# A gated attention and expert block: another order for the work of batch 0

## The chip, the core and the metric

The kernel runs on one core of a Trainium2 chip. The core has a matrix engine (TensorE, PE in the tables; its weight loads are listed apart as PEld), three engines for elementwise work (VectorE or DVE, ScalarE or ACT, GpSimd or POOL), and SyncE (SP), which here only issues transfers. Each engine carries out its own instructions in the order in which the program emits them; semaphores make one wait for another. Transfers are issued by SP, ACT or POOL and carried out by 16 DMA engines. The metric is the device time of one execution in microseconds; lower is better.

## The reference

Eight batches of 256 tokens of width 512, all in fp32. Each batch goes through an attention block and an expert block, both gated:

```python
x = x + jnp.tanh(g_xattn[0]) * _L0_xattn_ref(_layernorm(x, axis=-1), ctx_2048, ...)
x = x + jnp.tanh(g_ffn[0]) * _L0_ffn_ref(_layernorm(x, axis=-1), ...)

# attention: 32 query heads, 8 key heads of width 16, two sources of keys
q = _heads(jnp.concatenate([ssm_states, hidden_states], axis=-1) @ Wq, H)
k, v = _heads(hidden_states @ Wk, HK), _heads(hidden_states @ Wv, HK)
ssm_k, ssm_v = _heads(ssm_states @ Wsk, HK), _heads(ssm_states @ Wsv, HK)
...
scores = jnp.einsum('bhqd,bhkd->bhqk', q, k) / np.sqrt(D) + bias[None]   # ALiBi
scores = jnp.where(mask[None, None], scores, -jnp.inf)                  # 64 keys back, both sources
o = jnp.einsum('bhqk,bhkd->bhqd', jax.nn.softmax(scores, axis=-1), v)   # then @ Wo

# experts: 128 of them, each a mix of 8 basis products; top 4 a token
basis = jax.nn.silu((xt @ w_gate).reshape(T, K, I)) * (xt @ w_up).reshape(T, K, I)
mixed = jnp.einsum('tek,tki->tei', mix[topk_idx], basis)
out = jnp.einsum('teh,te->th', jnp.einsum('tei,ih->teh', mixed, w_down), topk_w * expert_scale[topk_idx])
out = out + jax.nn.silu(xt @ shared_w_gate) * (xt @ shared_w_up) @ shared_w_down
```

## The kernel before

**Stages of a batch.** `project(b)` makes keys, queries and values (PE, evicted by ACT). `attention(b)` does the softmax and the product with the values. `tail(b, t)`, for each half t of 128 tokens, multiplies by wo, adds the residual, normalises, transposes into hT and computes the router's choice. `feed_forward(b)` does the eight basis products and the shared expert. Stages of neighbouring batches run beside each other.

**The order** of all instructions is written by a planner in Python that stands at the end of the function (`start`, `run`). Every stage is a generator; it yields costs, and `start(gen, length, at, total)` places it on an axis where one batch is 1.0: a yield of cost c moves the stage on by c x length / total. `run` resumes whichever stage is due first, and what that stage then emits goes next into the engines' queues. Nothing is reordered afterwards, so a due time alone decides what stands behind what on each engine. Before the planner begins, loads, constants and the norm of batch 0 are emitted outside of this manual order.

**The softmax** of a batch has 8 groups of two query blocks, 16 units u in all (u = 2i + j). `score(i)` computes a group's scores for four pairs of key heads into four PSUM banks. A unit then takes `soften` for each pair (DVE: adds nbias, row extreme, L589), the exponential (ACT, L603), `divide` one unit later (DVE reciprocal, L612, then POOL, L615), `turn` two units later (DVE transpose, L623). After four units `values` (PE, L645) multiplies by vbd, and `take` (ACT, L662) evicts. `values` writes a spare part of the banks of a group's scores. A unit is emitted in four parts, with a yield of 1.0 behind each: the start, and steps 0, 1 and 2. The buffers `pr` that hold a unit's weights are three.

**vbd** holds the values on diagonals. `put_values` (ACT, L455) writes vpad, and `diagonals(qd, eng)` copies it by four transfers of 128 KB for each of four qd (L449), issued by `eng`.

**The feed-forward** multiplies two-by-two blocks with seven products instead of eight, which needs four sums of weight blocks for each k. For batch 0 they are formed once, stored to DRAM by `keep` (L848) and loaded from there by later batches. `first_sums(k)` forms the four sums of one k on POOL (`sub`, L844) while batch 0's attention runs: for k = 2, 3, 0, 1. Those of k = 4 to 7 are formed inside batch 0's feed-forward, two on DVE and two on POOL (`late`, `more`, L969). `load_gu` (L332) loads the weights, from SP.

**Banks.** Scores use a pool of four banks; batch 0's later groups also take two of the three feed-forward banks (`gu0` to `gu2`). One more bank (`one`) goes from user to user by `hold` and `give`.

## Time and profile before

| | us |
|---|---|
| median of three runs | 1043.92 (1040.56 to 1044.18) |
| profiled execution, its time | 1039.71 |
| profiled execution, its span | 1037.9 |
| PE busy in the span | 999.2 (96%) |
| DVE, ACT, POOL busy | 582.1, 420.5, 439.7 |
| first feed-forward matmul | 102.85 |

The span counts from the first to the last recorded instruction. The page gives each engine's busy time, then the chain of work that ended last, followed back from the end, then groups of instructions by source line. A row of a timeline has the start, the time from the first to the last of its instructions, engine, line, operation, output and inputs, and in brackets the idle time before it and what ended that. PE's ends are modelled, so neighbouring PE rows may overlap a little. In a group of PE matmuls the count is twice that of the source: each fp32 product is issued as two.

### The profile page before, as it was taken

What the parts mean: (1) busy time and instruction counts of PE and PEld (TensorE: products, weight loads), DVE (VectorE), ACT (ScalarE), POOL (GpSimd) and SP (SyncE); (2) the same over time, 40 slices, a digit from 0 to 9 for tenths busy, and PEclk for the clock granted to TensorE, in tenths of its full rate; (3) what the DMA queues carried; (4) which work ended last, traced back from release to release, by engine and by line L of the source; (5) the groups of instructions that cost most, each with busy time, mean ns of one, the idle gap of its engine ahead of it and who ended that gap; (6) DMA issues with size and microseconds to landing.
All of it is one profiled execution on the core that took longest, in us unless ns stands there. A gap on an engine that the chain in (4) does not pass through costs nothing.

```text
span 1037.9 us, 26745 instructions
## 1 busy us (share of the span) xinstructions
PE 999.2 (96%) x10072; PEld 793.6 (76%) x10072; DVE 582.1 (56%) x2185; ACT 420.5 (41%) x1608; POOL 439.7 (42%) x860
## 2 busy tenths in 40 slices
PE   6789989999999999999999999999999999999998
PEld 5657877867788688886878868787788868777885
DVE  1565666747554575536755467544756457754452
ACT  3452554426441464315543256423554136431220
POOL 3666456605542265413644136521454216540340
PEclk9889999999999999999999999999999999999999
DMA  8833964549543693527745386444954368553880
GB/s 254 217 109 115 234 186 150 174 129 283 163 137 111 169 300 123 159 98 191 263 138 157 107 235 217 144 136 125 278 163 144 112 166 258 167 174 120 263 277 20
DMA packets 111104, 180.80 MB, mean 174 GB/s; under 512 B 12160, under 2 KB 34176, under 8 KB 110976
## 3 DMA queue, kind: packets, MB, share of 16 engines
q1 hardware_dynamic: 108480, 176.22, 55.7%
q10 hardware_dynamic: 2112, 1.84, 0.5%
q8 instruction: 79, 1.29, 0.5%
q0 software_dynamic: 384, 1.05, 0.5%
q14 instruction: 49, 0.40, 0.1%
HBM read 149.69 MB, written 12.58 MB: 156 GB/s over the span
## 4 chain that ended last, share of the span: by engine, by line
PE 83%; DVE 8%; ACT 2%; DMA 2%; issue 2%; POOL 1%; SPq 1%; ACTq 0%; POOLq 0%; DVEq 0%
PE m L891 32%; PE ps L1025 10%; PE pq L512 8%; PE sc L645 5%; PE pd L1088 5%; PE po L758 5%; PE sc L576 5%; PE pd L1071 3%; PE pv L532 2%; PE pk L493 2%; DVE pr L589 2%; PE pl L789 1%; DVE pt L623 1%; ACT pr L603 1%; DMA w<-in_L_ffn_w_up 1%
## 5 line engine op out<-in xcount | busy, mean ns | idle before, releaser
L615 POOL TENSOR_SCALAR pr<-pr,rd 128x192 f32<-128x192 f32 (+2 forms) x512 | 206.5, 422 | 271.1 <-DVE rd L612 257.9
L603 ACT ACTIVATE pr<-pr,nm 128x192 f32<-128x192 f32 (+2 forms) x512 | 218.6, 430 | 109.8 <-DVE nm L589 73.8
L891 PE MATMUL m<-w,sT 128*128 128x256 f32 x1024 | 252.7, 381 | 0.1
L589 DVE CUSTOM_DVE_ANT_1 pr<-sc,nbias 128x192 f32<-128x192 f32 (+2 forms) x512 | 153.5, 322 | 122.9 <-PE sc L576 108.7
L891 PEld LDWEIGHTS m<-w,sT 128*128 128x128 f32 x1024 | 194.3, 191 | 27.7 <-issue 1.0
L891 PE MATMUL m<-w,hT 128*128 128x256 f32 x768 | 204.1, 388 | 0.0
L891 PEld LDWEIGHTS m<-w,hT 128*128 128x128 f32 x768 | 139.8, 191 | 24.2 <-issue 5.4
L964 POOL TENSOR_TENSOR mixed<-mixed,th 128x256 f32<-128x256 f32 x112 | 82.0, 732 | 177.3 <-DVE th L959 175.7
L1025 PE MATMUL ps<-hT,w 128*128 128x256 f32 x512 | 117.6, 381 | 0.0
L623 DVE STREAM_TRANSPOSE pt<-pr 128x768 f32<-128x768 f32 (+2 forms) x128 | 111.4, 871 | 3.3 <-POOL prob L798 1.9
L1025 PEld LDWEIGHTS ps<-hT,w 128*128 128x128 f32 x512 | 95.2, 190 | 14.7 <-issue 2.9
L603 ACT ACTIVATION_READ_ACCUMULATOR pr<-pr,nm 128x1 f32 x512 | 97.8, 191 | 0.0
L645 PEld LDWEIGHTS sc<-pt,vbd 64*32 64x32 f32 x5120 | 61.8, 106 | 27.5 <-issue 12.2
L645 PE MATMUL sc<-pt,vbd 64*32 64x96 f32 (+2 forms) x5120 | 70.9, 229 | 7.1 <-DMA vbd<-vpad 3.5
L576 PE MATMUL sc<-kT,qT 32*128 32x192 f32 (+2 forms) x1024 | 67.8, 343 | 6.3 <-DVE nm L589 6.0
L927 POOL TENSOR_TENSOR m<-m,u 128x256 f32<-128x256 f32 x64 | 47.7, 745 | 55.9 <-DVE u L926 47.0
L576 PEld LDWEIGHTS sc<-kT,qT 32*128 32x128 f32 x1024 | 48.2, 188 | 27.6 <-DVE nm L589 9.2
L949 DVE TENSOR_TENSOR gate<-u,m 128x256 f32<-128x256 f32 x64 | 26.4, 413 | 67.5 <-PE m L891 67.5
L854 ACT ACTIVATE th<-m 128x256 f32<-128x256 f32 x64 | 24.7, 386 | 96.6 <-DVE up L937 94.5
L854 ACT ACTIVATE th<-gate 128x256 f32<-128x256 f32 x64 | 26.5, 415 | 87.4 <-DVE gate L949 87.4
L758 PE MATMUL po<-wo,oT 128*128 128x512 f32 x128 | 57.7, 594 | 0.3 <-DVE cf L832 0.3
L512 PE MATMUL pq<-ctT,wq 128*128 128x256 f32 x224 | 54.2, 385 | 2.8 <-ACT kT L500 2.8
(129 smaller groups left out, 1212.8 us busy)
## 6 DMA issues: line engine op xcount, KB each, us to landing
w<-s SPq DMA_DIRECT2D x232, 256.0 KB, 3.3
w<-in_L_ffn_w_gate SPq DMA_DIRECT2D x132, 256.0 KB, 3.1
w<-in_L_ffn_w_up SPq DMA_DIRECT2D x74, 256.0 KB, 4.0
vbd<-vpad SPq DMA_DIRECT2D x120, 128.0 KB, 3.3
s<-w SPq DMA_DIRECT2D x32, 256.0 KB, 3.1
w<-in_L_ffn_shared_w_gate SPq DMA_DIRECT2D x32, 256.0 KB, 3.1
w<-in_L_ffn_shared_w_up SPq DMA_DIRECT2D x32, 256.0 KB, 2.9
ctT<-in_ctx SPq DMA_DIRECT2D x8, 512.0 KB, 5.7
```

The lines of the kernel that those rows point to most:

```text
L512: nc.tensor.matmul(pq, lhsT=wq_sb[:, c, g * P : (g + 1) * P], rhs=(ctT if c < NC else xnT)[:, c % NC, :], start=(c == 0), stop=(c == 2 * N ...
L576: nc.tensor.matmul(seen(scs[p][:, j * COLS : (j + 1) * COLS], qb), lhsT=qT[rows, qb].rearrange("p g q -> p (g q)"), rhs=kT[rows, par, :, f ...
L589: nc.vector.tensor_tensor_reduce(out=part, in0=seen(scs[p][:, j * COLS : (j + 1) * COLS], qb0 + j), in1=bass.AP(tensor=bias.tensor, offset ...
L603: nc.scalar.activation(part, part, AF.Exp, bias=nmax, scale=-1.0, accum_out=den)
L615: nc.gpsimd.tensor_scalar(part, part, rden[:, p : p + 1], 1.0, op0=ALU.mult, op1=ALU.mult)
L623: nc.vector.transpose(pt[:, u % 4].rearrange("p c (s k) -> p (c s) k", s=2)[:, :, lo:], pr.rearrange("p c (s k) -> p (c s) k", s=2)[:, :, ...
L645: nc.tensor.matmul(scs[gp][32 * c : 32 * (c + 1), 2 * COLS + lo * Q : 2 * COLS + hi * Q], lhsT=vbd[rows, kb % (P // Q), kb // (P // Q) * 2 ...
L758: nc.tensor.matmul(po, lhsT=oT[:, ch // 2, ch % 2, t * P : (t + 1) * P], rhs=wo_sb[:, ch % 2, ch // 2, :], start=(ch == 0), stop=(ch == 3),)
L891: nc.tensor.matmul(dst, lhsT=sides_of[m][c], rhs=w[:, c, :], start=(first and c == 0), stop=(c == NC // 2 - 1), skip_group_check=True,)
L964: nc.gpsimd.tensor_add(mixed[t], mixed[t], th)
L1025: nc.tensor.matmul(pg[:, j, :], lhsT=w[c // 2][:, c % 2, ic % 2 * P : (ic % 2 + 1) * P], rhs=hT[:, c, :], start=(c == 0), stop=(c == NC - 1),)
L1088: nc.tensor.matmul(po, lhsT=lhsT, rhs=rhs, start=False, stop=(j == len(inner) - 1))
```

## The change

**Loads.** The manual order now covers the whole function. SP loads batch 0's context and its first 128 tokens; everything else up to batch 1's inputs is issued by ACT, in the order in which it is used. Fourteen transposes of the identity and a tanh of a constant are emitted first. The four terms of nbias that the even groups use follow the first tile's norm, the other four the second's.

**Projections.** `project_first` emits what the first scores need and leaves the rest to a generator `rest`, which ends in `project(1)`. It is not on the planner's axis: batch 0's softmax calls `piece`, and each unit advances it by at most one piece of PE's work and one eviction. What is left when the softmax ends is emitted by `others`. The diagonals of batch 0 are issued by SP, ACT, POOL and SP.

**Softmax of batch 0** has its own loop, `first_batch`: scores of group i + 1 are emitted in step 1 of the second unit of group i; they rotate over six banks from the start; `values` of a set of four units goes into the banks of the group before, both halves in one unit.

**Sums and small weights.** The gates, wo, amplitudes, scale and router weights are loaded by `after_diagonals`, at -0.535, so behind the diagonals on SP. `first_sums` runs for k = 2, 0, 1; k = 3 joins those formed in the feed-forward. Batch 1's attention starts at -0.19 with length 0.86.

```diff
--- before.py
+++ after.py
+WARM = 14
...
+    ctx.enter_context(tc.manual_schedule())
...
-    def hold():
+    def hold(gap=GAP):
         me = object()
         queue.append(me)
-        while queue[0] is not me or now[0] < given[0] + GAP:
+        while queue[0] is not me or now[0] < given[0] + gap:
...
-    ctT_0 = load_context(0)
+    loaded[0] = x_0, load_context(0)
     wsk_sb = weight(wsk, HID, HK * D, "wsk", nc.scalar)
-    for t in range(NT):
-        nc.sync.dma_start(x_0[:, t, :], x[0, t * P : (t + 1) * P, :])
-    loaded[0] = x_0, ctT_0
+    nc.sync.dma_start(x_0[:, 0, :], x[0, :P, :])
     wq_sb = const.tile([P, 2 * NC, HID], F32, tag="wq", name="wq")
-    for half, eng in enumerate((nc.scalar, nc.sync)):
-        if half:
-            wk_sb = weight(wk, HID, HK * D, "wk", nc.scalar)
-        eng.dma_start(
+    def load_queries(half):
+        nc.scalar.dma_start(
             wq_sb[:, half * NC : (half + 1) * NC, :],
             wq[half * HID : (half + 1) * HID].rearrange("(c p) n -> p c n", p=P),
         )
+    load_queries(0)
+    wk_sb = weight(wk, HID, HK * D, "wk", nc.scalar)
+    nc.scalar.dma_start(x_0[:, 1, :], x[0, P:, :])
+    load_queries(1)
     wsv_sb = weight(wsv, HID, HK * D, "wsv", nc.scalar)
-    wv_sb = weight(wv, HID, HK * D, "wv", nc.sync)
-    loaded[1] = load(1), load_context(1)
+    wv_sb = weight(wv, HID, HK * D, "wv", nc.scalar)
+    loaded[1] = load(1, nc.scalar), load_context(1, nc.scalar)
...
+    warm = const.tile([P, 1], F32, tag="warm", name="warm")
+    nc.scalar.activation(warm, neghalf[:, :1], AF.Tanh)
+    idle = next_bank("idle")
+    for _ in range(WARM):
+        nc.tensor.transpose(idle[:, 0, :P], ident, ident)
...
+    first_normed = []
+    for t in range(NT):
+        first_normed += norm(loaded[0][0], [t], f"a0_{t}")()
+        for kv in ((4, 6, 0, 2), (5, 7, 1, 3))[t]:
+            nc.gpsimd.tensor_scalar(
+                nbias[:, kv], dist, slope, 2.0 ** (-8.0 * G * kv / H), op0=ALU.mult, op1=ALU.mult
+            )
...
+    def after_diagonals():
+        coef_in = other_weights()
+        yield 1.0
+        coefficients(*coef_in)
     def first_weights():
-        for k in (2, 3, 0, 1):
+        for k in (2, 0, 1):
             for g in range(1, 5):
                 load_gu(k, g)
             if k == 2:
                 later["wd"] = weight(w_down, I, HID, "wd", nc.sync)
                 later["sd"] = weight(sw_down[SI // 2 :], SI // 2, HID, "sd", nc.sync)
-            if k == 3:
+            if k == 0:
                 yield 2.0
                 yield from first_sums(2)
-                yield 1.0
-                yield from first_sums(3)
-        yield 3.0
+        yield 1.0
         yield from first_sums(0)
         yield 1.0
         yield from first_sums(1)
...
+    MORE = 1.8 + 1e-9
...
         pk = early("pk_0", 2)
         keys(pk, 0, slice(0, T))
+        evict = transposed(xnT, first_normed[0], 0, "x0", lambda shape, name: early(name, NC))
         pqs = [next_bank(f"pq_0_{g}")[:, 0, :P] for g in range(G - 1)]
         pqs.append(ps_one.tile([P, P], F32, tag="one", name="pq_0_3"))
         for g in range(G):
             queries(pqs[g], g, tiles[0], range(NC))
         put_keys(pk, 0, slice(0, T))
-        transposed(xnT, first_normed[0], 0, "x0", lambda shape, name: early(name, NC))()
+        evict()
+        evict = transposed(xnT, first_normed[1], 1, "x0", lambda shape, name: early(name, NC))
         keys(pk, 1, tiles[0])
         for g in range(G):
             queries(pqs[g], g, tiles[0], range(NC, 2 * NC))
         put_keys(pk, 1, tiles[0])
+        evict()
         for g in range(G):
             put_queries(pqs[g], g, 0)
         projected[0] = kT, qT
...
+        def rest():
...
+            pv = own("pv_0").rearrange("p (t s n) -> p t s n", t=NT, s=2)
+            for t in range(NT):
+                yield BEFORE if t == 0 else MORE
+                for s, (w_sb, src) in enumerate(((wsv_sb, ctT), (wv_sb, xnT))):
+                    for c in range(NC):
+                        nc.tensor.matmul(
+                            pv[:, t, s, :], lhsT=src[:, c, tiles[t]], rhs=w_sb[:, c, :],
+                            start=(c == 0), stop=(c == NC - 1),
+                        )
+            yield AFTER
+            put_values(pv)
+            for qd, eng in enumerate((nc.sync, nc.scalar, nc.gpsimd, nc.sync)):
+                diagonals(qd, eng)
+            yield BEFORE
+            pk = own("pk_0_1").rearrange("p (s n) -> p s n", s=2)
+            keys(pk, 1, tiles[1])
+            yield AFTER
+            put_keys(pk, 1, tiles[1])
+            normed = norm(loaded[1][0], range(NT), "a1")
+            for g in range(G):
+                yield BEFORE
+                pq = own(f"pq_0_{g}_1")[:, :P]
+                queries(pq, g, tiles[1], range(2 * NC))
+                yield AFTER
+                put_queries(pq, g, 1)
+                if g == 1:
+                    xns = normed()
+            ready.add("queries")
+            yield from project(1, xns)
+        fill.append(rest())
+        fill.append(next(fill[0]))
+    fill = []
+    def piece(*kinds):
+        if fill and (fill[1] in kinds or fill[1] not in (AFTER, BEFORE, MORE)):
+            fill[1] = next(fill[0], None)
+    def others():
+        while fill[1] is not None:
+            yield fill[1]
+            fill[1] = next(fill[0], None)
...
-            yield from hold()
+            yield from hold(0.0 if b == 1 else GAP)
...
+        if xns is None:
+            normed = norm(xt, range(NT), f"a{b}")
+            yield 3.0
+            xns = normed()
+            yield 3.0
         xnT = two.tile([P, NC, T], F32, tag="xo", name=f"xnT_{b}")
+        if b == 1:
+            yield BEFORE
...
-            yield AFTER
+            yield AFTER if s else MORE
...
-                    yield AFTER
+                    yield MORE if c < NC else AFTER
...
-            yield AFTER
+            yield AFTER if t else MORE
...
-            if b == 0 and taken[0] > 4 * NPAIR and taken[0] % 6 < 2:
-                return other_bank(taken[0] % 6, name)
+            if b == 0 and taken[0] % 6 in (5, 0):
+                return other_bank(int(taken[0] % 6 == 0), name)
             return ps_sc.tile([P, 2 * COLS + P], F32, tag="sc", name=name)
         def score(i):
             par, qb0 = groups[i]
-            scs = [bank(f"sc_{b}_{i}_{p}") for p in range(NPAIR)]
+            scs = [None] * NPAIR
+            for p in (2, 3, 0, 1):
+                scs[p] = bank(f"sc_{b}_{i}_{p}")
...
+        def first_batch():
+            scs = {0: score(0)}
+            for u in range(2 * n + 3):
+                i, j = divmod(u, 2)
+                m = u // 4 - 1 if u >= 6 and u % 4 == 2 else None
+                if m is not None:
+                    into = scs.get(i - 1) or [bank(f"sc_{b}_{i}_{p}") for p in range(2)]
+                    values(m, 0, pts[m], into)
+                exponentials()
+                if i < n:
+                    nmax = memory(u)
+                if m is None:
+                    piece(BEFORE, MORE)
+                yield 1.0
+                for step, ps in enumerate(((2,), (3,), (0, 1))):
+                    exponentials()
+                    for p in ps:
+                        if i < n:
+                            soften(i, j, p, scs[i], prs[u], nmax, dens[u])
+                    if step == 0 and m is not None:
+                        values(m, 1, pts[m], into)
+                        piece(BEFORE, MORE)
+                    if step == 1:
+                        if j == 1 and i + 1 < n:
+                            assert i + 1 < n // 2 or "queries" in ready
+                            scs[i + 1] = score(i + 1)
+                        if 0 <= u - 1 < 2 * n:
+                            divide((u - 1) // 2, (u - 1) % 2, prs[u - 1], dens.pop(u - 1))
+                    if step == 2:
+                        if 0 <= u - 2 < 2 * n:
+                            turn(u - 2)
+                        if m is not None:
+                            take(m, into)
+                            if m == n // 4 - 1:
+                                start(tail(b, 0, oT), 0.22, total=37.0)
+                        piece(AFTER)
+                    yield 1.0 if i < n else 0.3
+            start(tail(b, 1, oT), 0.16, total=37.0)
+            start(others(), 1.0, total=100.0)
+            yield 0.1
...
+        if b == 0:
+            yield from first_batch()
+            return
...
-            late = b == 0 and k > 3
-            more = b == 0 and 3 < k + 1 < NK
+            late = b == 0 and k > 2
+            more = b == 0 and 2 < k + 1 < NK
...
-    EARLY, FIRST = -0.2, -0.04
+    EARLY, FIRST = -0.2, -0.19
...
-    with tc.manual_schedule():
-        first = project_first()
-        next(first)
-        coef_in = other_weights()
-        start(attention(0), 0.42, at=-0.62, total=74.1)
-        start(first, 0.12, at=-0.615, total=7.1)
-        start(project(1), 0.54, at=-0.54, total=44.0)
-        start(first_weights(), 0.42, at=-0.52, total=25.0)
-        start(once(coefficients, *coef_in), 1.0, at=-0.46)
...
-            else:
-                start(attention(1), 0.74, at=max(at, FIRST), total=74.1)
...
+    project_first()
+    start(attention(0), 0.38, at=-0.585, total=70.0)
+    start(after_diagonals(), 0.13, at=-0.535, total=1.0)
+    start(first_weights(), 0.36, at=-0.53, total=16.0)
+    start(attention(1), 0.86, at=FIRST, total=74.1)
...
```

## The prediction

> **What bounds the kernel now.** I read the page first: TensorE is busy for 999.2 of 1037.9 us, and the chain that ended last lies on PE for 83%. So the time is TensorE's work plus what TensorE idles or loses to its clock, and an edit that leaves its work alone can only change that second part. The stage table shows where it lies (columns: stretch, length, busy time with count of PE, PEld, DVE, ACT, POOL, then granted clock, DMA share, GB/s):
>
> ```profile
> 0.00:21.00 21.00, 12.79 (x84) 11.10 (x84) 3.31 (x11) 4.45 (x10) 8.92 (x35) 1.00 0.96 291
> 21.00:38.00 17.00, 15.13 (x152) 14.05 (x153) 8.55 (x52) 10.30 (x47) 9.48 (x22) 1.00 0.53 106
> 38.00:44.00 6.00, 2.92 (x40) 2.10 (x39) 3.79 (x18) 2.79 (x13) 4.53 (x12) 0.99 1.07 206
> 44.00:61.00 17.00, 13.19 (x197) 9.75 (x202) 9.06 (x43) 7.88 (x34) 11.40 (x19) 0.50 0.64 237
> 61.00:86.00 25.00, 21.86 (x450) 16.62 (x435) 16.14 (x66) 15.13 (x61) 17.98 (x34) 1.00 0.38 138
> 86.00:103.00 17.00, 14.96 (x224) 11.27 (x215) 8.79 (x22) 1.90 (x7) 8.43 (x10) 1.00 0.22 81
> 103.00:237.00 134.00, 128.82 (x1312) 101.34 (x1314) 84.26 (x327) 59.67 (x234) 66.04 (x119) 1.00 0.61 175
> 237.00:1037.90 800.90, 789.56 (x7659) 627.35 (x7658) 448.19 (x1649) 318.43 (x1206) 312.90 (x612) 1.00 0.57 174
> ```
>
> Up to 103 us, where batch 0's feed-forward starts, PE is busy for 80.9 us: 22.1 idle. In 44 to 61 it runs at half clock, so 13.2 busy hold 6.6 of work: 6.6 lost. From 103 to 237 it idles 5.2, in the 801 us after that 11.3, which the change hardly touches.
>
> Then the timelines of PE and DVE up to 103:
>
> ```profile
> 5.42 3.78 PE L375 MATMUL pk<-ctT,wsk 128*128 128x256 f32 x8 [5.42 <-DMA wsk<-in_L_xattn_Wsk]
> 10.98 3.84 PE L388 MATMUL pq<-ctT,wq 128*128 128x128 f32 x32 [1.78 <-DMA wq<-in_L_xattn_Wq]
> 21.03 0.73 PE L576 MATMUL sc<-kT,qT 32*128 32x64 f32 x16 [0.37 <-ACT qT L396]
> ...
> 44.68 1.02 PE L645 MATMUL sc<-pt,vbd 64*32 64x96 f32 x46 [2.40 <-DMA vbd<-vpad]
> ...
> 61.44 1.99 PE L493 MATMUL pk<-xnT,wk 128*128 128x256 f32 x8
> ```
> ```profile
> 60.44 0.36 DVE L589 CUSTOM_DVE_ANT_1 pr<-sc,nbias 128x192 f32<-128x192 f32 x1 [3.91 <-PE sc L576]
> ...
> 69.12 0.36 DVE L589 CUSTOM_DVE_ANT_1 pr<-sc,nbias 128x192 f32<-128x192 f32 x1 [3.00 <-PE sc L576]
> ```
>
> The first eight matmuls take 3.78 us where eight of the same shape take 1.99 later: 1.8 lost to a cold clock that the column doesn't show. Total idle and lost before 103: 22.1 + 6.6 + 1.8 = **30.5 us**. The DVE rows show why the softmax stands still in 55 to 69: its scores sit in PE's queue behind whole projections at half clock. Last, SyncE's and GpSimd's timelines:
>
> ```profile
> 30.34 7.62 SPq L449 DMA_DIRECT2D vbd<-vpad  x8
> 38.01 1.85 SPq L332 DMA_DIRECT2D w<-in_L_ffn_w_gate  x2
> 39.90 1.30 SPq L332 DMA_DIRECT2D w<-in_L_ffn_w_up  x2
> ```
> ```profile
> 42.09 1.41 POOL L615 TENSOR_SCALAR pr<-pr,rd 128x128 f32<-128x128 f32 x4 [0.98 <-DVE rd L612]
> 46.49 1.27 POOL L844 TENSOR_TENSOR w<-w,w 128x512 f32<-128x512 f32 x1 [2.98 <-DMA w<-in_L_ffn_w_up]
> ```
>
> POOL runs the divisions of the softmax and the sums of the expert weights in one order; the first sum waits for a load that SP could issue only behind the eight diagonal copies.
>
> **Part by part, up to the first scores.** PE's first matmul still waits for wsk: 5.4 idle. The 14 warm-up transposes cost nothing: at twice the 0.11 us of a transpose of 128x128 (four in 0.45) they are 3.1 us, between the identity (1.4) and 5.42; without that cover they would be paid in full. They should give back 0 to 1.8; I take 1.8, as nothing else fills that stretch. The tanh only moves the 1.28 us table load to where ACT is idle. The nine loads on ACT's queue cost ACT some 0.55 each while it has nothing else. wq's first half is now preceded by 1 MB instead of sharing with its second half, so it stops binding (the trace moves some 380 GB/s there). Instead PE waits for the normed tile: x lands at 6.07 and 0.69 + 0.18 + 0.15 (DVE), 0.58 (POOL), 0.58 (DVE), 0.2 of hand-offs make 8.45. From there: transposes 0.66, queries 3.84, transposes 0.45, keys 0.9, queries 3.6, evictions and hand-offs 0.8: scores at 18.7, 2.3 earlier. Idle so far 5.4 + 1.1 + 0.8 = **7.3**.
>
> **Units 0 to 7.** ACT paces: 4 x 0.445 for a full unit, 4 x 0.335 or 0.385 for the four narrow ones, one eviction of 0.2 to 0.47, and once four diagonal issues of 0.6 (2.4 us in ACT's own order, with the exponentials queued behind). PE has 3 scores (2.6), values of two tiles (3.6), keys 0.9, four queries (7.2) and the first values product (2.2): 16.5 in the 18.5 us to 37.2: idle **2.0**. vpad is written at about 23 (before 30.25). The 16 diagonals are the same bytes; before, the DMA engines were 0.98 busy from 31 to 44.4, so I take 11 us, to 34, whichever queue issues them. Unit 6's values product sits in PE's queue behind that, with the scores of two units already done.
>
> **The new wait.** Moved behind the diagonals on SP are gates, wo, amp, escale and the router (nine issues; 11.4 to 19.2 before, where they hurt nobody). SP: diagonals till 30, these nine 5 to 7 us (a DMA also waits for an earlier one to land, as "wq" and "vbd" held SP's issues before), so the third load of the first sum is issued at 37 and lands 4 to 6.5 later: 42.5, against 46.35. POOL meets that sum ahead of unit 5's division (its due time, -0.4625, falls in unit 5; before it fell behind the division). Behind it wait the division, DVE's transpose of unit 5, and DVE's next units, which reach it at 37. Transposing starts at 42.5 + 1.27 + 1.41 = 45.2; before 51.33. From both sides: landing at 38 takes the wait away, at 49 (the longest landing of a diagonal, 9.2, on each round of queue waits) the gain too. PE, out of work from 39 to 45: idle **6**.
>
> **The clock.** [...] The row says more: after idle pieces of 0.5 and 2.4 us the clock stayed at 0.50 for 17 us and came back only after 5.9 us of unbroken matmuls (55.0 to 60.9). By that row as much as 8.5. PE now has a projection piece in each unit, so I take 8 us at half clock: **4** lost.
>
> **Units 8 to 17 and the tail.** Here PE decides. Per unit 0.45 score, 0.5 values, 1.73 projection = 2.7, and once the first tail (wo product 3.4, transposes, router 1.7): 32 for ten units, with the clock 36. POOL needs 1.62 for the division and at most one 1.27 sum: 2.9 a unit, 29. The third group of sums leaves this stretch (4 x 1.27 of POOL, 8 DMAs). Scores emitted half a group sooner remove the 3.9 and 3.0 us DVE waits; yet unit 5's transpose to unit 15's took 86.15 - 51.33 = 34.8 before, so this stretch gets no shorter: it takes in projections that lay elsewhere. The tail (values, wo product, norm, transposes) is 16.7 us before, 14 now, as PE has only the value projection and batch 1's first scores among it: idle **3**. Feed-forward from 45.2 + 0.9 + 36 + 14 = 96, not 103, with some 2 us more of batch 1's work done.
>
> **After it.** The sums of k=3 go into the feed-forward: 2 x 0.69 on DVE, 2 x 1.27 on POOL, 4 raw loads and 4 stores there, where it had 7 loads: 7 DMAs fewer in all. Their danger is the wait that k=4 shows: DVE stood 6.1 us for up-weights behind batch 1's diagonals, PE 3.4. Batch 1's attention starts 15 us earlier against the feed-forward, so the collision moves ahead of k=3's sums: from 3 us worse to 3.4 better; I take 1 better.
>
> **Sum.** 7.3 + 2 + 6 + 4 + 3 = 22.3 against 30.5: 8.2 (the start of the feed-forward by the chain, 7 earlier with 2 us of work ahead, agrees), plus 1: **9 us**. The profiled execution took 1039.7 (span 1037.9 and 1.8 around it), so 1030.5 for one like it; the three timed runs lie up to 4.5 above it, median 1043.92, so **1035**. Its own range, from the bounds above, is 1029 to 1040.
>
> **Rivals.** (A) The load lands by 38 and PE never idles long enough for the clock: 6 + 4 of cost vanish, less 2 of jitter: 1027. For it: DMA runs at 380 GB/s once the diagonals are through. Against: nine issues stand before it. (B) The gain turns into the new wait: the load lands at 47 to 49, softmax resumes at 50 to 52 as before, and only the first scores and the tail remain: 1042, no measurable change (a measurement of this kernel tells 0.5%, 5.2 us). For it: landings of 6.5 to 9.2 in that stretch. (C) Slower: the clock. If the gap of POOL's wait halves it and, as in 44 to 61, no unbroken stretch follows because each piece waits for the one bank's eviction, PE needs 5.4 us a unit. Each 2 us at half cost one beyond the 8 assumed; at 26 us the gain is gone, at 37 it is 0.5% slower; through the end of the softmax and tail (43 to 90, 47 us) it loses 23.5, not 4: 9 - 19.5, so 1054. For it: the 17 us of before. Against: PE's queue is denser now, and a full queue restores the clock.
>
> **Chances.** My case 0.52, A 0.15, B 0.18, C 0.15. Faster by over 0.5% (below 1038.7): most of my case (0.47), A, and a fifth of B: 0.66. Same: the rest of those and a little of C: 0.20. Slower 0.14. The range from 1024 to 1050 leaves out some 0.05 below and 0.12 above.
>
> **What would show it.** First scores near 18.7; one long wait of POOL's first sum for an up-weight, with DVE's transpose of unit 5 near 45; clock 0.50 for some 8 us behind it, not 17; no DVE wait on scores over 1 us after that; feed-forward from about 96; the 800 us behind 237 shorter by nothing. Wrong if that sum doesn't wait, if the clock stays low past 60, or if DVE stands at k=3's sums for over 6 us.

## The result, and the profile after

| | before | after |
|---|---|---|
| median of 20 runs each, us | 1040.18 (1037.26 to 1044.18) | 1045.81 (1040.99 to 1048.78) |
| ratio, with 95% interval | | 1.0049 (1.0035 to 1.0062) |
| profiled execution, its time | 1039.71 | 1040.99 |
| its span | 1037.9 | 1038.6 |
| first feed-forward matmul | 102.85 | 105.91 |

The change made the kernel 0.5% slower, 5.1 us, where 9 us faster was forecast. The profiled execution of after is the shortest of its 20 runs; a second one, in the last experiment, has a span of 1042.1 and the same stages.

The stage table of after (columns as before: stretch, length, busy time with count of PE, PEld, DVE, ACT, POOL, then granted clock, DMA share, GB/s):

```profile
0.00:21.00 21.00, 16.95 (x134) 15.65 (x135) 4.73 (x24) 6.29 (x21) 9.12 (x35) 1.00 0.76 250
21.00:38.00 17.00, 12.59 (x98) 11.76 (x97) 9.23 (x50) 8.37 (x40) 9.14 (x21) 0.81 0.80 163
38.00:44.00 6.00, 5.95 (x170) 5.33 (x169) 3.44 (x19) 2.92 (x15) 1.18 (x4) 0.97 1.09 278
44.00:61.00 17.00, 8.55 (x177) 6.40 (x177) 8.15 (x41) 8.76 (x36) 12.22 (x24) 0.70 0.69 245
61.00:86.00 25.00, 22.30 (x296) 16.31 (x297) 14.73 (x59) 14.15 (x57) 15.36 (x29) 1.00 0.14 50
86.00:103.00 17.00, 15.38 (x272) 11.45 (x271) 7.29 (x19) 2.65 (x10) 6.08 (x10) 1.00 0.13 48
103.00:237.00 134.00, 124.45 (x1275) 99.18 (x1276) 85.58 (x318) 56.61 (x221) 69.34 (x117) 0.97 0.59 171
237.00:1038.60 801.60, 790.43 (x7671) 627.36 (x7669) 451.12 (x1666) 320.98 (x1216) 315.05 (x618) 1.00 0.56 175
```

Up to 21 us PE gained; from 21 to 38 it is busy for 12.6 us at a clock of 0.81, where before it was busy for 15.1 at full clock; and 103 to 237, where before the clock was 1.00, now has 9.6 idle against 5.2, and a clock of 0.97. The same quantity as in the prediction, PE's idle time plus what it loses to the clock, summed over stretches of 2 us (in each the length less the busy time, plus the busy time times one less the clock; a stretch counts in the stage in which it starts), gives for the kernels spoken of below:

| stage, us | before | after | after again | E1 | E4 | E7 | E9 | E10 |
|---|---|---|---|---|---|---|---|---|
| 0 to 21 | 10.0 | 7.2 | 7.2 | 7.9 | 8.1 | 8.2 | 8.0 | 10.5 |
| 21 to 38 | 1.8 | 7.5 | 8.0 | 3.0 | 6.8 | 3.0 | 2.9 | 1.8 |
| 38 to 61 | 13.5 | 10.7 | 11.0 | 14.0 | 13.0 | 7.4 | 7.8 | 13.3 |
| 61 to 103 | 5.2 | 4.9 | 4.6 | 4.9 | 3.5 | 4.0 | 4.0 | 7.2 |
| 103 to 150 | 3.9 | 8.2 | 8.3 | 7.9 | 4.7 | 10.5 | 6.1 | 10.3 |
| 150 to 237 | 1.3 | 2.6 | 3.0 | 2.7 | 4.4 | 3.9 | 2.7 | 1.5 |
| sum | 35.7 | 41.1 | 42.1 | 40.4 | 40.5 | 37.0 | 31.5 | 44.6 |
| profiled span | 1037.9 | 1038.6 | 1042.1 | 1040.5 | 1041.0 | 1037.1 | 1030.9 | 1044.4 |

The first stage holds the 1.8 us of the cold first keys (3.78 us instead of 1.99) where there were any, and counts the warm-up transposes (3.1 to 3.3 us) as idle, since they are no work. Span less sum is 999.4 to 1000.5 in six columns; before and after depart from that by 2.2 and 2.5, so single sums are good to some 2.5 us. (Before lost 1.6 us to a clock of 0.91 at 917 to 937; the first profile of after had no such dip, the second had it.)

Up to 103 us the table has 30.5 before and 30.3 after: nothing of the forecast gain of 8.2 is there. Behind 103 it is 5.6 worse, where 1 better was forecast. PE's timeline shows the places:

```profile
5.68 1.99 PE L392 MATMUL pk<-ctT,wsk 128*128 128x256 f32 x8 [1.21 <-DMA wsk<-in_L_xattn_Wsk]
18.49 0.73 PE L631 MATMUL sc<-kT,qT 32*128 32x64 f32 x16 [0.37 <-ACT qT L413]
31.50 1.50 PE L631 MATMUL sc<-kT,qT 32*128 32x64 f32 x12 [4.41 <-DVE nm L644]
54.63 3.78 PE L546 MATMUL pk<-ctT,wsk 128*128 128x256 f32 x8 [7.44 <-ACT xnT L206]
133.72 1.55 PE L710 MATMUL sc<-pt,vbd 64*32 64x96 f32 x64 [5.42 <-DVE nm L644]
```

The first keys are warm and the first scores are out at 18.5, as forecast. Then three gaps of 4.4, 7.4 and 5.4 us, each followed by half clock: keys at 54.63 take 3.78 us instead of 1.99. The first gap is set off on ACT (first timeline). Behind the third stands a load that SP sent out (second). A row whose engine ends in "q" is a stretch of transfer issues:

```profile
23.70 3.67 ACTq L499 DMA_DIRECT2D vbd<-vpad  x4
27.41 0.40 ACT L663 ACTIVATE pr<-pr,nm 128x128 f32<-128x128 f32 x1 [3.75 <-issue]
```
```profile
103.68 2.56 SPq L499 DMA_DIRECT2D vbd<-vpad  x4
...
116.14 2.52 SPq L499 DMA_DIRECT2D vbd<-vpad  x4
122.74 0.38 SPq L348 DMA_DIRECT2D w<-in_L_ffn_w_up  x1
```

ACT's four diagonal issues took 3.67 us, not 2.4, and the exponential behind them starts only at 27.41; DVE's next row extremes wait for its buffer, and PE for those. On SP the raw up-weight for a sum of k = 3 goes out only at 122.74; batch 1's four sets of diagonals stand before it (E8 tests whether they hold it up). DVE's and then POOL's timelines:

```profile
47.67 0.71 DVE L688 STREAM_TRANSPOSE pt<-pr 128x512 f32<-128x512 f32 x1 [1.80 <-POOL pr L675]
52.18 0.16 DVE L310 TENSOR_REDUCE msum<-mix 128x1 f32<-128x8 f32 x1 [3.29 <-POOL mix L308]
59.51 0.36 DVE L644 CUSTOM_DVE_ANT_1 pr<-sc,nbias 128x192 f32<-128x192 f32 x1 [2.29 <-PE sc L631]
70.87 0.36 DVE L644 CUSTOM_DVE_ANT_1 pr<-sc,nbias 128x192 f32<-128x192 f32 x1 [3.87 <-PE sc L631]
128.68 0.69 DVE L948 TENSOR_TENSOR w<-w,w 128x512 f32<-128x512 f32 x1 [3.01 <-DMA w<-in_L_ffn_w_up]
```
```profile
44.97 1.27 POOL L948 TENSOR_TENSOR w<-w,w 128x512 f32<-128x512 f32 x1 [5.74 <-DMA w<-in_L_ffn_w_up]
46.23 1.41 POOL L675 TENSOR_SCALAR pr<-pr,rd 128x128 f32<-128x128 f32 x4
47.60 1.26 POOL L948 TENSOR_TENSOR w<-w,w 128x512 f32<-128x512 f32 x1
48.84 1.62 POOL L675 TENSOR_SCALAR pr<-pr,rd 128x192 f32<-128x192 f32 x4
50.43 1.26 POOL L948 TENSOR_TENSOR w<-w,w 128x512 f32<-128x512 f32 x1
...
51.94 0.20 POOL L308 TENSOR_TENSOR mix<-psq 128x8 f32<-128x8 f32 x1
```

The first sum waits 5.74 us for its up-weight, as forecast, and unit 5 is transposed at 47.67. What was not forecast stands behind it: the coefficients' product `mix` comes on POOL behind three sums and two divisions, DVE's reduction at 52.18 waits for it with all later softmax work behind it, ACT's exponential waits for DVE, and the eviction of batch 1's xnT, which PE wants at 54.63, stands behind that exponential. Of the third gap, from 128.3 to 133.72, DVE's wait fills only the start, up to 128.68. Then DVE works for 5 us on what had piled up behind the sum, a norm and a second sum among it, before PE gets its row extremes.

### The profile page after: what moved, and what is told of

The parts are those of the page before. It is cut to its first block, busy times and chain, and to the rows that moved or that the text cites. A ratio compares the mean times of both kernels' runs of the same rounds, so it can differ in the third digit from the quotient of the medians.

```text
span 1038.6 us, 26763 instructions
## 1 busy us (share of the span) xinstructions
PE 996.6 (96%) x10086; PEld 793.5 (76%) x10086; DVE 584.3 (56%) x2187; ACT 420.7 (41%) x1609; POOL 437.5 (42%) x854
## 3 DMA queue, kind: packets, MB, share of 16 engines
q8 instruction: 79, 1.29, 0.5%
## 4 chain that ended last, share of the span: by engine, by line
PE 84%; DVE 7%; DMA 3%; issue 3%; POOL 2%; ACT 1%; SPq 0%; POOLq 0%; DVEq 0%; ACTq 0%
PE m L995 33%; PE ps L1129 11%; PE pq L565 8%; PE sc L710 5%; PE pd L1192 5%; PE po L862 5%; PE sc L631 4%; PE pd L1175 3%; PE pk L546 3%; PE pv L585 2%; DVE pr L644 1%; PE pl L893 1%; DMA w<-in_L_ffn_w_up 1%; POOL pr L675 1%; POOL w L948 1%
## 5 line engine op out<-in xcount | busy, mean ns | idle before, releaser
L710 PE MATMUL sc<-pt,vbd 64*32 64x64 f32 (+2 forms) x5120 | 68.0, 228 | 7.0 <-DVE nm L644 5.4
L631 PE MATMUL sc<-kT,qT 32*128 32x192 f32 (+2 forms) x1024 | 65.0, 338 | 6.2 <-DVE nm L644 5.8
L1031 POOL TENSOR_TENSOR m<-m,u 128x256 f32<-128x256 f32 x64 | 48.8, 762 | 48.6 <-DVE u L1030 41.3
```

The lines of the kernel that those rows point to most:

```text
L631: nc.tensor.matmul(seen(scs[p][:, j * COLS : (j + 1) * COLS], qb), lhsT=qT[rows, qb].rearrange("p g q -> p (g q)"), rhs=kT[rows, par, :, f ...
L710: nc.tensor.matmul(scs[gp][32 * c : 32 * (c + 1), 2 * COLS + lo * Q : 2 * COLS + hi * Q], lhsT=vbd[rows, kb % (P // Q), kb // (P // Q) * 2 ...
```

## The experiments

All are edits of after unless said otherwise. "Against after" is the difference of the two ratios to before, times 1040 us.

**E1: the early copies off ACT.** Half of batch 0's diagonals are issued by SP and half by POOL.

```diff
-            for qd, eng in enumerate((nc.sync, nc.scalar, nc.gpsimd, nc.sync)):
+            for qd, eng in enumerate((nc.sync, nc.sync, nc.gpsimd, nc.gpsimd)):
```

> The changed kernel with one edit: batch 0's sixteen diagonal copies are issued by SP, SP, POOL, POOL as before, none by ACT. Theory A (ACT's own issues, 3.67 us, and the 4.4 us of PE idle and the halved clock behind them set the time): 4 to 7 us faster than the changed kernel, ratio to the kernel before 0.998 to 1.001. Theory B (the load of the first weight sum sets it; what comes sooner only waits longer there): the first POOL sum stays within 2 us of 45 us, the softmax resumes as late, and the time is within 2 us of the changed kernel, ratio 1.003 to 1.007. POOL pays 2.4 us more for its own issues in both.

1046.07 us, ratio 1.0052 (1.0036 to 1.0069): 0.3 us against after, nothing. Yet the gap is gone. Windows of E1, then POOL's timeline:

```profile
21.00:38.00 17.00, 14.05 (x148) 12.28 (x147) 11.47 (x62) 11.02 (x53) 12.44 (x29) 1.00 0.72 154
38.00:61.00 23.00, 13.72 (x302) 11.48 (x302) 9.43 (x50) 9.73 (x42) 12.03 (x24) 0.70 0.77 246
```
```profile
45.58 1.27 POOL L948 TENSOR_TENSOR w<-w,w 128x512 f32<-128x512 f32 x1 [8.45 <-DMA w<-in_L_ffn_w_up]
```

From 21 to 38 the clock is whole and the loss falls from 7.5 to 3.0; from 38 to 61 it rises from 10.7 to 14.0, since POOL's sum starts when its load lands, now after 8.45 us. The two waits are in series, and here the second takes up what the first gives back. (E1's first keys took 3.78 us, not 1.99, but that cost only 0.7 us up to 21.)

**E2: the nine small loads early.** The gates, wo, amplitudes, scale and router weights are loaded ahead of the diagonals.

```diff
+    coef_in = other_weights()
     start(attention(0), 0.38, at=-0.585, total=70.0)
...
     def after_diagonals():
-        coef_in = other_weights()
         yield 1.0
```

> The changed kernel with one edit: gates, wo, amplitudes, scale and router weights are issued on SP right after the first loads, ahead of the diagonal copies, as before. Theory B (the first sum's load is late because nine small transfers and their waits stand in front of it): the third load lands 4 to 6 us sooner, the first POOL sum runs near 40 us, PE's 7.4 us of idle behind it shrinks to 3 or less; 4 to 7 us faster than the changed kernel, ratio 0.998 to 1.001. Theory A: little moves, as the softmax isn't there yet; under 2 us. Theory C (PE's pieces and ACT's evictions in one order set the pace of the softmax): the gain is lost again before 103 us; under 2 us.

1044.96 us, ratio 1.0043 (1.0029 to 1.0056), 0.6 us against after. The first sum starts at 43.83 after a wait of 0.24 instead of 5.74. But the loads delay the second half of wq: PE waits 2.93 us for it until 12.32, and the first scores come at 22.90 instead of 18.49. The wait moved ahead.

**E5: E1 and E2 together**, the same lines as in both:

```diff
-            for qd, eng in enumerate((nc.sync, nc.scalar, nc.gpsimd, nc.sync)):
+            for qd, eng in enumerate((nc.sync, nc.sync, nc.gpsimd, nc.gpsimd)):
...
+    coef_in = other_weights()
```

> The changed kernel with both single edits of before together: diagonal copies from SP and POOL, none from ACT, and the nine small transfers ahead of them. Theory S (the waits of the first 60 us stand in series; one taken away only lengthens the next, so only several together gain): softmax unit 5 is transposed near 43 us instead of 47.7, PE idle and lost clock in 21 to 61 us fall from 18 to about 11 us, and of these 7 us some 4 are lost again to the second half of wq, which the small transfers delay as seen alone; 2 to 5 us faster than the changed kernel, ratio 1.000 to 1.003. Rival P (from unit 6 on PE's own work sets the pace and takes back what is won before): the same time as the changed kernel, within 1.5 us.

1045.30 us, ratio 1.0048 (1.0033 to 1.0063): no change. The first sum starts at 42.78 and unit 5's transpose at 47.73, no sooner than in after.

**E6: the coefficients later.** Only their due time moves, from -0.405 to -0.335, so POOL's `mix` and DVE's reduction fall behind unit 6's and 7's softmax.

```diff
-    start(after_diagonals(), 0.13, at=-0.535, total=1.0)
+    start(after_diagonals(), 0.2, at=-0.535, total=1.0)
```

> The changed kernel with one edit: the coefficients (two tiny POOL products and five tiny DVE steps) fall due at -0.335 instead of -0.405, so behind unit 11 instead of unit 8. In the trace of the changed kernel DVE stood 3.3 us there for POOL, which was still working off its backlog, and PE idled 7.4 us behind it. Theory S: unit 6 is transposed near 50.5 instead of 54.1, 3 to 4 us faster than the changed kernel, ratio 1.001 to 1.002. Rival P: PE's idle only moves, under 1.5 us.

1041.70 us, ratio 1.0013 (1.0001 to 1.0025): 3.7 us better than after, with intervals apart (that of after's second series, below, it just touches). PE's timeline of E6:

```profile
31.42 1.50 PE L631 MATMUL sc<-kT,qT 32*128 32x64 f32 x12 [4.23 <-DVE nm L644]
50.49 3.38 PE L546 MATMUL pk<-ctT,wsk 128*128 128x256 f32 x8 [4.28 <-ACT xnT L206]
```

The second gap is 4.28 instead of 7.44, and batch 1's keys come 4.1 us sooner, with the first gap untouched.

**E7: the sums later too.** E1 and E6, and the sums of k = 2, with those of k = 0 and 1 behind them, due later by two more divisions. **E11** is the same with ACT's copies left as in after.

```diff
             if k == 0:
-                yield 2.0
+                yield 4.0
                 yield from first_sums(2)
```

> The changed kernel with three edits that take the waits of the first 60 us away together: diagonal copies from SP and POOL, the first sums of weights due two units later (behind the division of unit 6) with their loads where they were, and the coefficients due at -0.335. Theory S: POOL no longer stands in front of a division, unit 6 is transposed near 44 us instead of 54, PE idle and lost clock in 21 to 61 us fall from 18 to 6 us or less; 8 to 12 us faster than the changed kernel, ratio 0.993 to 0.998. Rival P: the softmax runs ahead but PE's pieces and the end of the batch don't; under 3 us.

> The version that took the early waits away, with ACT issuing its four diagonal copies again. In the changed kernel itself these copies cost nothing, since what they delayed waited for the first sum anyway. Theory S (waits in series): with the sum out of the way they cost what their row says, ACT's 3.7 us of issuing and PE's 4.4 us of idle with the clock behind it: 3 to 5 us slower than that version, ratio 1.000 to 1.002. Rival P (PE's own work from unit 6 on takes it in): within 1.5 us, ratio 0.996 to 0.998.

E7: 1037.11 us, ratio 0.9969 (0.9956 to 0.9983), 8.3 us better than after and faster than before. E11: 1038.51 us, ratio 0.9975 (0.9960 to 0.9990). PE's timeline of E7:

```profile
35.48 1.12 PE L631 MATMUL sc<-kT,qT 32*128 32x192 f32 x12 [1.68 <-DVE nm L644]
47.13 3.20 PE L546 MATMUL pk<-ctT,wsk 128*128 128x256 f32 x8 [1.58 <-ACT xnT L206]
```

The first sum now starts without a wait for its load, at 46.24, behind unit 6's division. Of both gaps less than 1.7 us is left, and the feed-forward starts at 98.05. E11 keeps the first gap (5.34 us before 32.43) and ends 0.6 us behind E7, within the intervals; its profiled span is 1.9 us longer. So the due times of coefficients and sums were worth some 8 us, and ACT's copies nothing that these intervals can tell from zero. With the sum out of the way, waits in series would have made the copies cost 3 to 5 us. They did not, and what takes up PE's gap in E11 is not shown.

**E3: batch 1's attention back to its old start**, so that its diagonals do not precede k = 3's sums.

```diff
-    EARLY, FIRST = -0.2, -0.19
+    EARLY, FIRST = -0.2, -0.04
...
-    start(attention(1), 0.86, at=FIRST, total=74.1)
...
+        if b == 0:
+            start(attention(1), 0.74, at=max(at, FIRST), total=74.1)
```

> The changed kernel with one edit: batch 1's attention starts as before (at -0.04 or when the feed-forward starts, length 0.74) instead of at -0.19. Theory D (the early start puts batch 1's sixteen diagonal copies in front of the raw weights of k=3, whose sum then holds DVE for 3 us and PE for 5.4 us near 130 us, with the clock halved behind it): that idle goes, PE idle in 103 to 237 falls from 9 to about 5 us; 4 to 7 us faster than the changed kernel. If the sums of k=3 as such are the cause, the wait stays and the time is within 2 us. If the early start was worth its place, 2 to 4 us slower.

1050.57 us, ratio 1.0097 (1.0067 to 1.0127): 5.0 us worse than after. DVE still waits for an up-weight, 7.10 us until 136.73, and PE idles 6.43. The early start is worth some 5 us, and the collision does not come from it.

**E8: SP kept free.** Batch 1's sixteen diagonals are issued by POOL.

```diff
-                            diagonals(2 * (u - 1) + step, nc.sync)
+                            diagonals(2 * (u - 1) + step, nc.gpsimd if b == 1 else nc.sync)
```

> The changed kernel with one edit: batch 1's sixteen diagonal copies are issued by POOL instead of SP. Theory Q (the raw weights of k=3 are late because SP issues them behind those copies): the loads land 6 us or more sooner, the 5.4 us of PE idle near 130 us and the halved clock behind it go, 4 to 6 us faster than the changed kernel, less what 10 us of issuing cost POOL. Theory R (the 16 DMA engines are full there, whoever issues): the wait stays within 2 us, and the time is that of the changed kernel or slower.

1045.68 us, ratio 1.0058 (1.0041 to 1.0075): no better. DVE's timeline of E8, and then of after the transfers from 100 to 135 us (busy tenths of the DMA engines in 40 slices of 0.875 us):

```profile
130.24 0.69 DVE L948 TENSOR_TENSOR w<-w,w 128x512 f32<-128x512 f32 x1 [2.40 <-DMA w<-in_L_ffn_w_gate]
```
```profile
DMA  0000378868899999999989999999999999971000
```

The wait is there with SP free of diagonals, and PE idles 5.00 us behind it, until 135.29; POOL's sixteen issues took 8.9 us besides. So the diagonals in SP's order are not the cause. In after the DMA engines are busy for 0.9 or more from 110 to 131, but for one slice; E10 shows that this alone is not the cause either.

**E4: k = 3's sums back into the softmax**, the rest of the change kept.

```diff
-        for k in (2, 0, 1):
+        for k in (2, 3, 0, 1):
...
-            if k == 0:
+            if k == 3:
                 yield 2.0
                 yield from first_sums(2)
-        yield 1.0
+                yield 1.0
+                yield from first_sums(3)
+        yield 3.0
         yield from first_sums(0)
...
-            late = b == 0 and k > 2
-            more = b == 0 and 2 < k + 1 < NK
+            late = b == 0 and k > 3
+            more = b == 0 and 3 < k + 1 < NK
...
-    start(first_weights(), 0.36, at=-0.53, total=16.0)
+    start(first_weights(), 0.42, at=-0.53, total=25.0)
```

> The changed kernel with one part undone: the sums of k=3 are formed on POOL in batch 0's softmax again, at the pace of before, and not in the feed-forward. Theory D' (forming k=3's sums in the feed-forward costs the wait near 130 us): PE idle in 103 to 237 falls from 9 to 5 us or less, 3 to 6 us faster there, of which POOL's four more sums take back 0 to 3 before 103 us. If the early attention is the cause, the wait only moves to k=4's sums: within 2 us of the changed kernel, or slower.

1042.18 us, ratio 1.0013 (0.9999 to 1.0027): 3.7 us better than after. The loss from 103 to 150 falls from 8.2 to 4.7 and in no window of that stretch is the clock lowered; in 38 to 61 it rises from 10.7 to 13.0, where the first sum now waits 9.19 us for its load.

**E10: the kernel before with k = 3's sums alone moved into the feed-forward.**

```diff
-        for k in (2, 3, 0, 1):
+        for k in (2, 0, 1):
...
-            if k == 3:
+            if k == 0:
                 yield 2.0
                 yield from first_sums(2)
-                yield 1.0
-                yield from first_sums(3)
-        yield 3.0
+        yield 1.0
...
-            late = b == 0 and k > 3
-            more = b == 0 and 3 < k + 1 < NK
+            late = b == 0 and k > 2
+            more = b == 0 and 2 < k + 1 < NK
```

> The kernel before with one part of the change alone: the sums of k=3 are formed in batch 0's feed-forward, not in its softmax. If that part is a loss by itself, as undoing it in the changed kernel says: 3 to 5 us slower than before, ratio 1.003 to 1.005, with a DVE wait for a raw weight load and PE idle of some 5 us in the feed-forward of k=2. If it lost only in company with the early start of batch 1's attention: no change, 0.998 to 1.001, as POOL is freed of 5 us in the softmax.

1050.44 us, ratio 1.0090 (1.0055 to 1.0124): 9.4 us slower than before by this part alone. DVE's and then PE's timeline of E10:

```profile
135.18 0.69 DVE L842 TENSOR_TENSOR w<-w,w 128x512 f32<-128x512 f32 x1 [6.17 <-DMA w<-in_L_ffn_w_up]
```
```profile
137.33 1.12 PE L178 MATMUL tr_x<-ident,xn_a 128*128 128x128 f32 x4 [3.82 <-DVE xn_a L164]
140.40 2.07 PE L889 MATMUL m<-w,sT 128*128 128x256 f32 x4 [1.96 <-DVE th L857]
```

DVE stands 6.17 us, PE 3.82 and 1.96, and its products behind that run at half clock (0.50 from 138 to 142 us). In the stage table 103 to 150 goes from 3.9 to 10.3; its profiled span is 6.5 us longer. The other 3 of the 9.4 are not in that profile. Busy DMA engines alone don't make this loss. Windows of before, then of E10, and a row of DVE in before:

```profile
110.00:140.00 30.00, 27.70 (x234) 22.54 (x233) 20.77 (x90) 16.41 (x67) 15.35 (x32) 1.00 1.01 267
```
```profile
110.00:140.00 30.00, 23.55 (x134) 18.78 (x132) 18.28 (x70) 11.88 (x49) 16.16 (x27) 0.88 0.96 255
```
```profile
137.46 0.69 DVE L844 TENSOR_TENSOR w<-w,w 128x512 f32<-128x512 f32 x1 [4.76 <-DMA w<-in_L_ffn_w_up]
```

Before moved more in these 30 us (267 GB/s against 255), and its DVE waited for an up-weight too, of k = 4. But PE had other work to do meanwhile and idled 2.3 us, where in E10 it idled 6.5 and lost clock. So the loss depends on what PE has left when DVE stands; why that was less with k = 3's sums was not tested.

**E9: all three cures.** E7 with k = 3's sums in the softmax: E4's edit with two other yields. Against E4, besides the lines of E1 and E6:

```diff
             if k == 3:
-                yield 2.0
+                yield 6.0
                 yield from first_sums(2)
                 yield 1.0
                 yield from first_sums(3)
-        yield 3.0
+        yield 2.0
```

> The version that took the early waits away (copies from SP and POOL, first sums and coefficients later), and the sums of k=3 in batch 0's softmax as before, begun behind the division of unit 6. If the two losses are separate and add up (4 us for the waits of the first 60 us and their clock beyond the changed kernel's loss, 3.7 us for k=3's sums in the feed-forward): 3 to 4 us faster than that version, ratio to the kernel before 0.992 to 0.995, PE idle in 125 to 150 us 2 us instead of 5 to 6, no halved clock there. Rival: four more sums of 1.27 us and the stores in front of the loads of k=0 and k=1 hold POOL and cost it again before 103 us: ratio 0.996 to 0.999.

1033.20 us (1029.90 to 1036.38), ratio 0.9920 (0.9888 to 0.9952): 8.3 us faster than before and 13.4 than after, the shortest of all. Windows of E9:

```profile
38.00:61.00 23.00, 18.54 (x323) 14.45 (x324) 10.77 (x54) 13.38 (x56) 15.49 (x31) 0.85 0.68 225
...
125.00:150.00 25.00, 24.20 (x255) 19.92 (x254) 16.07 (x54) 13.01 (x47) 15.40 (x24) 0.97 0.51 164
```

From 125 to 150 PE idles 0.8 us, in after 5.7. Four more sums and their loads fit into the softmax at hardly any loss in 38 to 61 (7.8 against E7's 7.4). One wait for an up-weight stays, just ahead of that last window and on PE itself:

```profile
123.62 2.07 PE L997 MATMUL m<-w,sT 128*128 128x256 f32 x4 [3.77 <-DMA w<-in_L_ffn_w_up]
```

So 103 to 150 still loses 6.1, against 10.5 in E7 and 3.9 in before.

**After again:** the unchanged kernel, for a second profile.

> The changed kernel once more, for a second profile: the first profiled execution, 1041.0, lies 4.8 below the median of 1045.8. If its stages are those of an ordinary execution, the stage sums of idle and lost time up to 237 us come out within 2 of 7.2, 7.5, 10.7, 4.9, 8.2 and 2.6. If an ordinary execution is longer for a place in the order of the work, one of these stages is longer by 3 to 5; the candidates are the first keys at half clock (1.8, as in most variants of this kernel) and the values product behind the sums of k = 3. If the 4.8 lie in halved stretches behind 237 us, the stages agree and the clock of the whole run is 0.984 to 0.987 instead of 0.988.

1045.39 us, ratio 1.0041 (1.0024 to 1.0058). Its stages agree with the first profile within 0.5 us each, so they are no accident of one execution. The extra length lies behind 237 us (805.1 against 801.6). Of it 1.6 is a dip of the clock to 0.91 at 917 to 937, which the profile of before has too, and another 0.8 is idle. The clock of the whole run is 0.987.

## Why the prediction was wrong

The direction was wrong; the median lies inside the range, on its slow side. The range was wide, and the three runs that it started from had a median 3.7 us above that of all 20.

Two steps failed: the chain of waits before 103 us, which left out the coefficients, and the effect on the feed-forward, which was taken as a gain. By the table, 0.2 us of the 8.2 arrived before 103, and behind it came 5.6 worse instead of 1 better. By the runs, the first was worth about 8 us (E7, E11) and the second 3.7 to 5.1 (E4; E9 against E7). With both undone E9 gains 8.3, near the 9 of the forecast. None of the forecast's three signs of being wrong came: the first sum did wait, the clock was back before 60, and DVE stood for 3.0 us at k = 3's sums, not for 6.

**Up to the first scores (7.3): right.** Measured 7.2, first scores at 18.49 against 18.7.

**Units 0 to 7 (2.0): wrong, 7.5.** ACT's issues were named as lying in front of the exponentials, but priced at 0.6 each; they took 0.92. SP's row in the prediction (7.62 us for eight) had 0.95 already. PE's gap of 4.41 us was followed by half clock (a mean of 0.81 from 21 to 38 us), which the term left out. Yet E1 and E11 show that this term is not what made the kernel slower: without ACT's copies after was 0.3 us slower, and E11 0.6 faster. In E1 the wait for the first sum came after them in series, and a sum of terms counts such a wait in full where the chain counts it once. In E11 that wait is gone, and why the copies cost so little there stays open.

**The new wait and its clock (6 + 4): the first step that failed.** Stretch 38 to 61 cost 10.7, but that this is near 10 is luck: E7, without the wait, still loses 7.4 there. The 8 us at half clock were the author's estimate; PE worked 4.2 us at half clock behind the gap. The first sum started at 44.97 against 42.5 and unit 5's transpose came at 47.67 against 45.2, still sooner than before. But the next, unit 6's, came at 54.06, where before it was 53.37: here the early gain was used up. The step had listed what waits behind POOL's sum (division, transpose, later units) and left out the coefficients, which the same generator moves behind the small loads. E6 shows this wait at 3.7 us, E7 and E11 it and the sum's at about 8.

**Units 8 to 17 and the tail: too short.** Unit 5's transpose to unit 15's took 40.4 us, not 36.9. The first part of it is the wait just named. Its last part, units 6 to 15, took 34.0, 33.8 in E7, and 32.8 before, so nothing in this part made the kernel much slower. DVE's waits for scores did not fall under 1 us (2.29 and 3.87 above): a score still stands behind wo's product. From the last transpose to the feed-forward it took 17.9, not 14; PE does value pieces and batch 1's scores there, so little of that is idle: 4.9 us from 61 to 103, where 3 were forecast. The 2.5 at unit 5, 3.5 and 3.9 make up the 10 us by which the feed-forward starts later than forecast.

**After it ("I take 1 better"): the second step that failed, and it turned the sign.** It gave 3 worse to 3.4 better, from k = 4's wait and a collision that would move ahead of k = 3's sums. It moved onto them. By the stage table the cost is 4.3 to 150 us and 1.3 to 237, by E4 3.7, in the kernel before by itself 9.4. The step counted seven transfers fewer, and measured the danger by the wait at k = 4 (DVE 6.1 us, PE 3.4). At k = 3 DVE waited only 3.01 us and PE lost more, 5.42 in one gap and half clock for 3.6 us behind it: what stood behind the sum in DVE's order, and what PE had left to do meanwhile, were not looked at. E8 shows that another issuing engine doesn't help; E3 shows that no late start of batch 1 does.

**Rivals.** B (gain turned into a new wait, about 1042) comes nearest up to 103 us, though the load landed at 45, not at 47 to 49. C's long half-clock stretch did not come; PE worked at half clock for 6.8, 4.2 and 3.6 us after the three gaps. A would have needed no wait. None of them had the feed-forward's own loss, which tips the result to the slow side.

## What to carry to other kernels

Before moving work to a later stage, list what will stand behind it on its engine there, and what the other engines have left to do while it waits: DVE's wait for k = 3's load was 3.0 us, PE's gap 5.4 with 3.6 us of half clock on top. The DMA share doesn't tell this: the kernel before had 1.01 in that stretch and kept its clock. When a load moves behind others, list every later instruction of the generator that it belongs to, small ones first: a reduction of 0.16 us held DVE for 3.3 and cost the kernel 3.7 (E6). And where waits stand in series, look for the last: curing earlier ones gave nothing (E1; E2 and E5 too, though their loads also delayed wq).

## What the runs showed of the hardware

**Half clock outlasted each of the three gaps.** Windows of after, one for each return of the full clock:

```profile
38.00:39.00 1.00, 1.00 (x9) 1.00 (x9) 1.00 (x5) 0.45 (x3) 0.94 (x4) 0.83 1.05 239
58.00:59.00 1.00, 1.00 (x13) 0.66 (x16) 0.00 (x0) 0.00 (x0) 0.17 (x1) 0.59 1.01 277
137.00:138.00 1.00, 1.00 (x5) 0.86 (x4) 1.00 (x4) 0.74 (x4) 1.00 (x2) 0.84 0.00 0
```

A clock of 0.83 in 1 us means half clock for 0.34 us of it, so the returns are near 38.3, 58.8 and 137.3 us. In windows of 0.1 us, with 1.00 before and 0.50 behind, the falls are near 31.5, 48.6 and 130.5. Counted from the end of each gap (4.41, 7.44 and 5.42 us), full clock came back after 6.8, 4.2 and 3.6 us of work without a pause, so the longest gap did not have the longest stretch behind it. So a gap of 4 to 7 us should be priced at 3.6 to 6.8 us of half clock behind it, a loss of 1.8 to 3.4 us, as an estimate from these three.

**The warm-up did not always work.** The fourteen transposes, always 3.1 to 3.3 us from 1.37, left the first keys at 1.99 us in both profiles of after, in E2 and in E11, but at 3.57 to 3.78 in E1 and in E3 to E9, where PE's pause before the keys was the same 1.0 to 1.3 us. So four of twelve profiles had the gain of some 1.8 us. What decides this is not shown, and nothing in the record ties it to the edits.

**Half clock doesn't double every product.** In the profile before, a values product of 64 matmuls took 1.29 us at 46.68, at clock 0.50, and 0.89 at 63.36, at full clock; the keys took 3.78 against 1.99.
